# A running maximum for the widest tiles of a graph attention kernel, layer 1

## The chip, the cores and the metric

The kernel runs on one core of a Trainium2 chip. The time is device microseconds of one execution, smaller is better. The core has a matrix engine (PE, whose weight loads are shown apart as PEld), a vector engine (DVE), a scalar engine (ACT), a general engine (POOL), which in this kernel mostly issues gathers, and a queue engine (SP), all of which run their own instruction lists in order and wait for each other by semaphores. Sixteen DMA engines move data between the main memory and the on-chip memories (SBUF for data, PSUM for what the matrix engine sums).

## The reference

A graph has N = 10000 nodes and 170000 directed edges (80000 random ones in both directions, and a loop at each node). `x` has 768 numbers a node. Two graph attention layers follow each other, then a residual sum and a last layer norm. Layer 1 has 4 heads of 256 numbers, layer 2 one head of 768:

```
xl    = (x @ W).reshape(n, heads, out_ch)
e     = leaky_relu(alpha_src[src] + alpha_dst[dst], 0.2)
m     = segment_max(e, dst)
e     = exp(e - m[dst])
s     = segment_sum(e, dst)
alpha = e / (s[dst] + 1e-16)
out   = segment_sum(xl[src] * alpha[:, :, None], dst)      # then + bias
h     = relu(layer_norm(out)) + (x @ Wr1 + br1)            # layer 1
h     = layer_norm(out2) + (h1 @ Wr2 + br2)                # layer 2
x     = layernorm(x + h)
```

So every node takes a softmax over the edges that end in it, for each head, and a weighted sum of the source nodes' rows. Subtracting the maximum changes nothing but the range of the exponential; a softmax may therefore also be taken over groups of edges, if sums made with an older, smaller maximum are scaled by exp(old maximum − new maximum).

## The kernel before

A first stage (until about 900 us) computes `xl` and the two attention terms of every node, writes them as rows of 1033 floats into a table in main memory (`table1`: 1024 numbers, 4 + 4 attention terms, 1 rank), and sorts the nodes by their number of edges. Then layer 1 (about 900 to 3440 us) and layer 2 (to the end) work through 79 tiles of 128 nodes. A tile has a fixed number of slots, the most edges that a node of it may have: slot k of a tile is a gather of 128 table rows, one a partition, the k-th neighbour of each of the 128 nodes. The text calls such a gathered slot a **row** of the tile, and a tile's place in the order of work its **turn**. The slot counts, computed in `slot_counts`, rise from 8 in turn 0 to a peak in the middle and fall to 9 in turn 78. Turns 33 to 46 have 21, 22, 22, 23, 24, 26, 41, 27, 25, 24, 23, 22, 22 and 21 rows; no other turn has more than 21.

Rows live in a ring of `RING1 = 29` slots in SBUF, shared by consecutive turns (class `Ring`). `ring.fetch` issues the gather for ring position q on POOL as soon as position q − 29 has been used, in the order of work; line 424 is that gather.

A turn of at most 29 rows goes through the loop of `ordered_layer1` (lines 772 to 875):

- `weights_of(t)`: `logits` over all its rows (lines 477 to 489: sum of the attention terms, leaky ReLU, maximum over the rows, difference, `exp` on ACT, two small writes into `slots` and the ring), then `normalised` (doubled loop weight, sum, reciprocal, product; lines 496 to 502), then `summed`, in two halves: ACT scales a unit matrix by the weights (`diagonals`, line 727) and PE multiplies the first `on_pe(t)` rows (4 in the wide turns) with them into a PSUM tile `acc` (line 733).
- `weigh` adds the other rows to `acc` on DVE: one row in four as 4 instructions of 256 numbers, one a head, that multiply and add (line 519); of the other three ACT has scaled the row in the ring before (`multiply`, line 508), and DVE adds 1024 numbers in one instruction (line 515).
- The turn before is finished at the beginning of the loop: mean and deviation of its `acc` (`deviation`, lines 577 to 582), then `scaled` and the residual (lines 591, 593, 804), transposes, and products for layer 2.

The order in each engine's list is the order in which the code emits it. `weights_of(t + 1)` is a generator: its first piece, the logits, is emitted at row n − 3 of turn t (`LEAD` is 3), its second (normalisation and the first half of the sums) at row n − 2, the rest after the deviation at the beginning of turn t + 1. This needs all rows of turn t + 1 in the ring while 3 rows of turn t are still unused, hence the condition `SLOTS[t + 1] + LEAD <= ring.size`.

The one turn with 41 rows, turn 39, does not fit. It goes through `attend_parts`: 3 groups of 13, 14 and 14 rows with a running maximum; each group has its own logits, 4 rows on PE into a PSUM tile `sums`, the others into a tile `h` in SBUF, which is scaled by `fade = exp(top − new)` at each new group (line 543). Turn 39 isn't prepared during turn 38, nor turn 40 during turn 39.

Of the kernel before, what the change touches and what calls it, by code (L numbers as in the profile page):

```python
# [35 lines left out]
P = 128  # L36
# [14 lines left out]
ON_PE2 = 512  # L51
SHARE = 4
ON_PE1 = 4


def chunk_counts(n_edges):
# [23 lines left out]
def gnn_kernel(ctx, tc, x, x_cols, src, dst, src_col, dst_col, W1, a_src1, a_dst1, b1, g1, be1, Wr1, br1,  # L80
# [390 lines left out]
    def logits(small, ring, lo, hi, ad, heads, c, top=None):  # L471


        n = hi - lo
        e = small.tile([P, ring.size, heads], F32, name="e")[:, :n]
        for a, b, rows in ring.parts(lo, hi):
            nc.vector.tensor_tensor(e[:, a - lo:b - lo], rows[:, :, c + heads:c + 2 * heads],
                                    ad[:, None, :].to_broadcast([P, b - a, heads]), op=OP.add)
# [22 lines left out]
    def doubled(e, t):  # L501
        nc.vector.tensor_scalar(e[:, 0], e[:, 0], loops[:, TURNS[t]:TURNS[t] + 1], None, op0=OP.mult)

    def multiply(row, e, dh):

        for h in range(e.shape[1]):
            s = slice(h * dh, (h + 1) * dh)
            nc.scalar.activation(row[:, s], row[:, s], AF.Copy, scale=e[:, h:h + 1])  # L508

    def weigh(acc, row, e, dh, first=None, shared=False):  # L510


        if shared:
            c = e.shape[1] * dh
            nc.vector.tensor_add(acc[:, :c], acc[:, :c], row[:, :c])  # L515
            return
        for h in range(e.shape[1]):
            s = slice(h * dh, (h + 1) * dh)
            nc.vector.scalar_tensor_tensor(acc[:, s], row[:, s], e[:, h:h + 1],  # L519
                                           (acc if first is None else first)[:, s], op0=OP.mult, op1=OP.add)  # L520

    def attend_parts(small, ring, acc, h_, ad, heads, dh, t, summed, between):


        c = heads * dh
        groups = -(-SLOTS[t] * 2 // ring.size)
        cuts = [FIRST[t] + SLOTS[t] * g // groups for g in range(groups + 1)]
        top = total = sums = None
        nc.vector.memset(acc[:, :c], 0.0)
        for lo, hi in zip(cuts, cuts[1:]):  # L530
            e, new = logits(small, ring, lo, hi, ad, heads, c, top)
            if lo == FIRST[t]:
                doubled(e, t)
            part = small.tile([P, heads], F32, name="part")
            nc.vector.reduce_sum(part, e.rearrange("p k h -> p h k"), axis=AX.X)
            if top is not None:
                nc.vector.tensor_add(acc[:, :c], acc[:, :c], sums[:, :c])
                fade = small.tile([P, heads], F32, name="fade")
                nc.vector.tensor_sub(fade, top, new)
                nc.scalar.activation(fade, fade, AF.Exp)  # L540
                for h in range(heads):
                    s = slice(h * dh, (h + 1) * dh)
                    nc.vector.tensor_scalar(acc[:, s], acc[:, s], fade[:, h:h + 1], None, op0=OP.mult)
                nc.vector.tensor_mul(fade, total, fade)
                nc.vector.tensor_add(part, part, fade)
            top, total = new, part
            m = min(ON_PE1, hi - lo - 1)
            pe = lo if hi == cuts[-1] else hi - m
            steps = summed(pe, e[:, pe - lo:], m)
            sums = next(steps)  # L550
            if pe == lo:
                for _ in steps:
                    pass
            alone = [q for q in range(lo, hi) if not pe <= q < pe + m]
            for k, q in enumerate(alone):
                shared = k >= len(alone) // 3
                if shared:
                    multiply(ring.slot(q), e[:, q - lo], dh)
                if k == len(alone) // 3 + 1:
                    for _ in steps:  # L560
                        pass
                weigh(acc, ring.slot(q), e[:, q - lo], dh, shared=shared)
                ring.fetch(q + 1 + ring.size)
            ring.fetch(hi + ring.size)
            between.pop(0)()
        nc.vector.tensor_add(acc[:, :c], acc[:, :c], sums[:, :c])
        divided(small, h_, acc, total, None, heads, dh)

    def pieces(a, width):

# [112 lines left out]
    def ordered_layer1():  # L683
        nc.scalar.add_instruction(mybir.InstLoadActFuncSet(name=nc.get_next_instruction_name(), act_func_set_id=6, engine=nc.scalar.engine))
        with tc.tile_pool(name="b1", bufs=1) as pool, tc.tile_pool(name="small1", bufs=2) as small, \
# [32 lines left out]
            def on_pe(t):  # L718


                return min(max(SLOTS[t] // 2 - 5, 1), ON_PE1, SLOTS[t])

# [14 lines left out]

            def weights_of(t):

                n, m = SLOTS[t], on_pe(t)  # L740
                e, _ = logits(small, ring, FIRST[t], FIRST[t] + n, ring.slot(FIRST[t])[:, C1:C1 + H1], H1, C1)
                yield e
                normalised(small, e, H1, t)
                acc = ps_acc.tile([P, 2 * BANK], F32, name="acc")
                diagonals = pool.tile([P, ON_PE1 * H1, P], F32, name="diagonals")
                for lo, hi in ((0, min(m, 2)), (min(m, 2), m)):
                    summed(acc, diagonals, e, FIRST[t], lo, hi, m)
                    yield acc

            def shared(t, k):  # L750
                return (k - on_pe(t)) % SHARE > 0
# [20 lines left out]
            for t in range(NT + 1):  # L772
                live, events = t < NT, []
                n = SLOTS[t] if live else 0
                first = done = on_pe(t) if live else 0
                whole = live and n <= ring.size
                if whole and not ready:
                    ahead = weights_of(t)
                    ready += itertools.islice(ahead, 2)

                def multiplied(upto):
                    nonlocal done
                    while whole and done < min(upto, n):
                        if shared(t, done):
                            multiply(ring.slot(FIRST[t] + done), e[:, done], DH1)
                        done += 1

                if whole:
                    e, acc = ready
                if last:  # L790
                    r_before, means = last
                    stats = deviation(small, pieces(means[:, :C1], BANK))
                for _ in ahead:
                    pass
                if full is not None:
                    store(t - 2)
                moves = []
# [15 lines left out]
                    if live and t:  # L813
                        r = product(xT, wr1, C1, ps_r)

                if whole:
                    by_wr1()

                def to_layer2():
                    nonlocal full  # L820
# [20 lines left out]
                    while events and events[0][0] <= k:  # L841
                        events.pop(0)[1]()

                if live and not whole:
                    due(first + 1)
                    sums, acc = (ps_acc.tile([P, 2 * BANK], F32, name="acc") for _ in range(2))
                    ad = small.tile([P, H1], F32, name="ad")
                    nc.vector.tensor_copy(ad, ring.slot(FIRST[t])[:, C1:C1 + H1])

                    def some(q, e, m):  # L850
                        diagonals = pool.tile([P, ON_PE1 * H1, P], F32, name="diagonals")
                        for lo, hi in ((0, min(m, 2)), (min(m, 2), m)):
                            summed(sums, diagonals, e, q, lo, hi, m)
                            yield sums

                    h = pool.tile([P, C1], F32, name="h")
                    attend_parts(small, ring, h, acc, ad, H1, DH1, t, some,
                                 [by_wr1, lambda: due(n)] + [lambda: None] * n)
# [12 lines left out]
                due(DEGREES)  # L871
# [414 lines left out]
```

## Time and profile before

| | us |
|---|---|
| median of 3 runs | 5645.9 (5635.85 to 5646.04) |
| profiled execution | 5629.25, span 5627.4 |
| DVE busy in the span | 4288.7 (76%) |
| ACT / POOL / PE busy | 2810.9 / 3236.3 / 4889.5 |
| turns 33 to 45 (between the starts of their line 804) | 1879.92 to 2468.02, 588.1 |
| DVE busy in each 36 to 47 us turn there | 32 to 38 |
| turn 39 (41 rows) | 2128.45 to 2208.79, 80.34 |

Line 804 is emitted once a turn, so the time from one to the next is the length of a turn. A row of a timeline gives the start, the duration, the engine, the line, the operation, what it writes and reads, how often it follows itself, and in brackets how long the engine had been idle and what released it. Where equal instructions follow each other the duration is that of all of them.

### The profile page before, as it was taken

How to read it: one execution, taken by the hardware profiler on the slowest of the kernel's cores; microseconds unless marked ns; L12 is line 12 of the kernel's file. 1: busy time of each engine (PE TensorE's matmuls, PEld its weight loads, DVE VectorE, ACT ScalarE, POOL GpSimd, SP SyncE). 2: the span in 40 equal slices, each digit the busy share in tenths (PEclk: the TensorE clock that was granted, in tenths of full speed). 3: DMA queues.
4: the chain of work that ended last, by engine and by line, in shares of the span. 5: the costliest groups of instructions: out<-in, count | busy, mean ns of one | idle time of the engine just before them, and what ended most of it. 6: DMA issues, size and time to landing. Idle time of an engine off the chain costs nothing. (4 is left out here: it accounts for less than half of the span.)

```text
span 5627.4 us, 59568 instructions
## 1 busy us (share of the span) xinstructions
PE 4889.5 (87%) x15191; PEld 2895.8 (51%) x15191; DVE 4288.7 (76%) x7729; ACT 2810.9 (50%) x8184; POOL 3236.3 (58%) x3159
## 2 busy tenths in 40 slices
PE   8999996999999875789999999998887747788898
PEld 3444443555555543455555555565555534555565
DVE  5783344999998887888999995887676656767787
ACT  3443343777788776778877763332222222222232
POOL 2447364556666555566665543666565656666663
PEclk9999998999999987899999999998888878889999
DMA  4333626999999987899999986998888878888885
GB/s 155 122 99 87 92 89 243 327 338 350 361 363 364 347 318 263 317 346 357 366 356 354 337 292 246 330 337 313 294 301 286 282 242 291 307 300 305 304 328 201
DMA packets 474306, 1591.37 MB, mean 283 GB/s; under 512 B 118327, under 2 KB 122487, under 8 KB 473958
## 3 DMA queue, kind: packets, MB, share of 16 engines
q0 software_dynamic: 322384, 1286.62, 64.5%
q1 hardware_dynamic: 149520, 297.43, 15.7%
q10 hardware_dynamic: 2054, 3.42, 0.2%
q8 instruction: 128, 2.10, 0.1%
q14 instruction: 220, 1.80, 0.1%
HBM read 1431.80 MB, written 177.29 MB: 286 GB/s over the span
## 5 line engine op out<-in xcount | busy, mean ns | idle before, releaser
L424 POOL DMA_INDIRECT ring<-table,slots x2675 | 2655.8, 993 | 1791.0 <-issue 518.8
L519 DVE SCALAR_TENSOR_TENSOR acc<-ring,e,acc 128x512 f32<-128x512 f32 (+1 forms) x2530 | 1578.4, 624 | 148.0 <-PE acc L733 48.6
L508 ACT ACTIVATE ring<-ring,e 128x256 f32<-128x256 f32 x3284 | 1338.6, 508 | 1.4 <-issue 1.4
L515 DVE TENSOR_TENSOR acc<-acc,ring 128x1024 f32<-128x1024 f32 x801 | 985.6, 1230 | 71.4 <-DVE acc L519 1.4
L952 PE MATMUL big<-wr,w 128*128 128x512 f32 (+1 forms) x2464 | 878.9, 502 | 139.8 <-issue 137.9
L938 PE MATMUL big<-ring,diagonals 128*128 128x256 f32 x2754 | 742.1, 428 | 206.0 <-issue 159.2
L171 PE MATMUL big<-w,xT 128*128 128x512 f32 x1896 | 825.9, 597 | 27.0 <-DMA w<-in_W_dram 10.4
L171 PE MATMUL big<-wr,xT 128*128 128x512 f32 x1896 | 833.5, 596 | 0.2 <-issue 0.2
L826 PE MATMUL half<-w,hT 128*128 128x512 f32 (+1 forms) x2528 | 830.4, 486 | 0.0
L938 PEld LDWEIGHTS big<-ring,diagonals 128*128 128x128 f32 x2754 | 586.4, 216 | 364.9 <-issue 232.7
L952 PEld LDWEIGHTS big<-wr,w 128*128 128x128 f32 x2464 | 482.3, 197 | 499.9 <-issue 468.9
L937 ACT ACTIVATE diagonals<-ident,e 128x128 f32<-128x128 f32 x1377 | 424.3, 388 | 617.2 <-remote 227.0
L826 PEld LDWEIGHTS half<-w,hT 128*128 128x128 f32 x2528 | 477.8, 189 | 372.3 <-issue 333.2
L733 PE MATMUL acc<-ring,diagonals 128*128 128x256 f32 x1912 | 481.8, 410 | 209.4 <-ACT diagonals L727 203.8
L171 PEld LDWEIGHTS big<-w,xT 128*128 128x128 f32 x1896 | 362.0, 192 | 486.6 <-issue 466.3
L171 PEld LDWEIGHTS big<-wr,xT 128*128 128x128 f32 x1896 | 356.7, 192 | 420.6 <-issue 420.5
L733 PEld LDWEIGHTS acc<-ring,diagonals 128*128 128x128 f32 x1912 | 388.8, 206 | 295.4 <-ACT diagonals L727 225.0
L581 ACT ACTIVATE sd<-mv,eps 128x1 f32<-128x1 f32 x237 | 69.4, 293 | 709.9 <-DVE mv L579 398.4
L727 ACT ACTIVATE diagonals<-ident,e 128x128 f32<-128x128 f32 x956 | 293.0, 387 | 204.2 <-DVE e L499 171.9
L665 DVE TENSOR_TENSOR scr<-big,ad_b 128x1024 f32<-128x1024 f32 x79 | 96.7, 1224 | 379.9 <-ACT row L662 348.1
L670 POOL TENSOR_TENSOR row<-row,none 128x1024 f32<-128x1024 f32 x79 | 187.1, 2368 | 266.6 <-ACT row L662 264.6
L485 ACT ACTIVATE e<-e 128x68 f32<-128x68 f32 (+29 forms) x160 | 38.2, 239 | 567.0 <-DVE e L484 302.0
(173 smaller groups left out, 3635.0 us busy)
## 6 DMA issues: line engine op xcount, KB each, us to landing
ring<-table,slots POOLq DMA_INDIRECT x2675
table<-row SPq DMA_DIRECT2D x79, 516.0 KB
h_d<-hT SPq DMA_DIRECT2D x79, 512.0 KB
w<-h_d SPq DMA_DIRECT2D x77, 512.0 KB
table<-row SPq DMA_DIRECT2D x79, 385.0 KB
ring<-table SPq DMA_DIRECT2D x79, 385.0 KB
xT<-in_x_cols_dram SPq DMA_DIRECT2D x79, 384.0 KB
x_d<-xt SPq DMA_DIRECT2D x79, 384.0 KB
```

The costliest lines, as they stand in the source:

```text
L171: nc.tensor.matmul(p[:, c:e], aT[:, j, :], w[:, j, c:e], start=(j == 0), stop=(j == k - 1))
L424: nc.gpsimd.indirect_dma_start(out=to, out_offset=None, in_=table, in_offset=bass.IndirectOffsetOnAxis(ap=index, axis=0), **more)
L508: nc.scalar.activation(row[:, s], row[:, s], AF.Copy, scale=e[:, h:h + 1])
L515: nc.vector.tensor_add(acc[:, :c], acc[:, :c], row[:, :c])
L519: nc.vector.scalar_tensor_tensor(acc[:, s], row[:, s], e[:, h:h + 1], (acc if first is None else first)[:, s], op0=OP.mult, op1=OP.add)
L670: nc.gpsimd.tensor_add(row[:, :C1], row[:, :C1], b1_b)
L727: nc.scalar.activation(diagonals[:, k * H1 + i, :], ident, AF.Copy, scale=e[:, k, i:i + 1])
L733: nc.tensor.matmul(acc[:, c:d], diagonals[:, k * H1 + i, :], ring.slot(q + k)[:, c:d], start=(k == 0 and c % BANK == 0), stop=(k == m - 1 ...
L826: nc.tensor.matmul(q, hT[:, j, :], w2[:, j, c:c + q.shape[1]], start=(j == 0), stop=(j == K1 - 1))
L937: nc.scalar.activation(diagonals[:, k % G, :], ident, AF.Copy, scale=e[:, k, :])
L938: nc.tensor.matmul(to, diagonals[:, k % G, :], ring.slot(FIRST[t] + k)[:, ON_PE2:C2], start=False, stop=(k == n - 1), skip_group_check=True)
L952: nc.tensor.matmul(r[:, c:d], hT[:, j, :], wr2[:, j, c:d], start=False, stop=(j == K1 - 1 and d < C2), skip_group_check=True)
```

## The change

A threshold `PARTED = 22` is added. Tiles with 22 rows or more take their softmax in groups of rows: two groups, or three for the 41 rows. `cuts_of(t)` gives the borders: 11 for 22 and 23 rows, 13 for 24 to 27 rows, 13 and 27 for 41 rows (a border that would fall on a row not scaled by ACT moves on by one).

`weights_of` takes the logits of the first group only, and gives unnormalised weights; the sums of the four rows on PE go into `acc` with these. For each later group at row c it has two more pieces: the logits with the old maximum, and `fade`, emitted at row c − 8; then the running total, and for the last group the reciprocal, which is multiplied into the group's weights and into its `fade`, emitted at row c − 5. At row c `weigh` does acc = acc · fade + row, 4 instructions of 256 numbers, in place of one addition of 1024 numbers. All sums stay in the PSUM tile `acc`. `attend_parts` goes; turn 39 runs through the same loop as the others, and every turn is prepared during the one before it, whatever its size. Turns under 22 rows have one group and the instructions of before.

```diff
+PARTED = 22
@@ weigh
-    def weigh(acc, row, e, dh, first=None, shared=False):
+    def weigh(acc, row, e, dh, first=None, shared=False, fade=None):
+        if fade is not None:
+            for h in range(e.shape[1]):
+                s = slice(h * dh, (h + 1) * dh)
+                nc.vector.scalar_tensor_tensor(acc[:, s], acc[:, s], fade[:, h:h + 1], row[:, s],
+                                               op0=OP.mult, op1=OP.add)
+            return
@@ attend_parts is removed
-    def attend_parts(small, ring, acc, h_, ad, heads, dh, t, summed, between):
...
@@ weights_of
-                n, m = SLOTS[t], on_pe(t)
-                e, _ = logits(small, ring, FIRST[t], FIRST[t] + n, ring.slot(FIRST[t])[:, C1:C1 + H1], H1, C1)
-                yield e
-                normalised(small, e, H1, t)
+                n, m, at = SLOTS[t], on_pe(t), FIRST[t]
+                cuts = cuts_of(t)
+                ad = ring.slot(at)[:, C1:C1 + H1]
+                if len(cuts) > 2:
+                    own = ad
+                    ad = small.tile([P, H1], F32, name="ad")
+                    nc.vector.tensor_copy(ad, own)
+                e, top = logits(small, ring, at, at + cuts[1], ad, H1, C1)
+                yield {0: (e, None)}
+                if len(cuts) == 2:
+                    normalised(small, e, H1, t)
+                else:
+                    doubled(e, t)
+                    total = small.tile([P, H1], F32, name="total")
+                    nc.vector.reduce_sum(total, e.rearrange("p k h -> p h k"), axis=AX.X)
...
+                for lo, hi in zip(cuts[1:], cuts[2:]):
+                    e, new = logits(small, ring, at + lo, at + hi, ad, H1, C1, top)
+                    fade = small.tile([P, H1], F32, name="fade")
+                    nc.vector.tensor_sub(fade, top, new)
+                    nc.scalar.activation(fade, fade, AF.Exp)
+                    yield
+                    part = small.tile([P, H1], F32, name="part")
+                    nc.vector.reduce_sum(part, e.rearrange("p k h -> p h k"), axis=AX.X)
+                    nc.vector.tensor_mul(total, total, fade)
+                    nc.vector.tensor_add(total, total, part)
+                    top = new
+                    if hi == n:
+                        nc.vector.tensor_scalar(total, total, 1e-16, None, op0=OP.add)
+                        nc.vector.reciprocal(total, total)
+                        nc.vector.tensor_mul(fade, fade, total)
+                        nc.vector.tensor_mul(e, e, total[:, None, :].to_broadcast([P, hi - lo, H1]))
+                    yield lo, (e, fade)
+
+            def cuts_of(t):
+                n = SLOTS[t]
+                groups = 1 if n < PARTED else -(-2 * n // ring.size)
+                cuts = [n * g // groups for g in range(groups + 1)]
+                return [c + (0 < c < n and not shared(t, c)) for c in cuts]
@@ the loop over turns
-                for _ in ahead:
-                    pass
+                next(later, None)
...
-                if whole and t + 1 < NT and SLOTS[t + 1] + LEAD <= ring.size:
+                if live and t + 1 < NT:
                     ahead = weights_of(t + 1)
-                for k in range(n if whole else 0):
+                for k in range(n):
+                    if k + 2 * LEAD + 2 in cuts[1:-1]:
+                        next(later)
+                    if k + LEAD + 2 in cuts[1:-1]:
+                        lo, es_lo = next(later)
+                        es[lo] = es_lo
                     multiplied(k + 1 + LEAD)
                     if n - LEAD <= k < n - LEAD + 2:
                         ready += itertools.islice(ahead, 1)
                     if k >= first:
-                        weigh(acc, ring.slot(FIRST[t] + k), e[:, k], DH1, shared=shared(t, k))
+                        weights, fade = row_of(k)
+                        weigh(acc, ring.slot(FIRST[t] + k), weights, DH1, shared=shared(t, k), fade=fade)
```

More of the change, by code (lines that the diff above doesn't have):

```diff
@@ L520, in weigh @@
                                            (acc if first is None else first)[:, s], op0=OP.mult, op1=OP.add)
-    def attend_parts(small, ring, acc, h_, ad, heads, dh, t, summed, between):
[L525 to L552, printed above, removed]
-                    pass
[L554 to L567, printed above, removed]
     def pieces(a, width):
@@ L746, in weights_of @@
                 for lo, hi in ((0, min(m, 2)), (min(m, 2), m)):
-                    summed(acc, diagonals, e, FIRST[t], lo, hi, m)
+                    summed(acc, diagonals, e, at, lo, hi, m)
                     yield acc
+                for lo, hi in zip(cuts[1:], cuts[2:]):
[20 more added lines that the diff above has]
+                return [c + (0 < c < n and not shared(t, c)) for c in cuts]
             def shared(t, k):
@@ L775, in ordered_layer1, with row_of @@
                 first = done = on_pe(t) if live else 0
-                whole = live and n <= ring.size
-                if whole and not ready:
+                cuts = cuts_of(t) if live else []
+                if live and not ready:
                     ahead = weights_of(t)
                     ready += itertools.islice(ahead, 2)
+                def row_of(k):
+                    lo = max(c for c in es if c <= k)
+                    return es[lo][0][:, k - lo], es[lo][1] if k == lo else None
                 def multiplied(upto):
                     nonlocal done
-                    while whole and done < min(upto, n):
+                    while done < min(upto, n):
                         if shared(t, done):
-                            multiply(ring.slot(FIRST[t] + done), e[:, done], DH1)
+                            multiply(ring.slot(FIRST[t] + done), row_of(done)[0], DH1)
                         done += 1
-                if whole:
-                    e, acc = ready
+                later = iter(())
+                if live:
+                    es, acc = ready
+                    es, later = dict(es), ahead
                 if last:
@@ L792, in ordered_layer1 @@
                     stats = deviation(small, pieces(means[:, :C1], BANK))
-                for _ in ahead:
-                    pass
+                next(later, None)
                 if full is not None:
@@ L814, in by_wr1 @@
                         r = product(xT, wr1, C1, ps_r)
-                if whole:
-                    by_wr1()
+                by_wr1()
                 def to_layer2():
@@ L842, in due @@
                         events.pop(0)[1]()
[L844 to L858, printed above, removed]
                 ready = []
                 ahead = iter(())
-                if whole and t + 1 < NT and SLOTS[t + 1] + LEAD <= ring.size:
+                if live and t + 1 < NT:
                     ahead = weights_of(t + 1)
-                for k in range(n if whole else 0):
+                for k in range(n):
[4 more added lines that the diff above has]
+                        es[lo] = es_lo
                     multiplied(k + 1 + LEAD)
```

## The prediction

> **What bounds the kernel now.** The chain that ended last says nothing here: its pieces cover the last microsecond only. So I looked at the share of each engine, then at windows cut turn by turn, then at the waits of the turns that the change touches, then at the timeline of single turns. Windows first (columns: stretch, length, busy time and instruction count of PE, PEld, DVE, ACT, POOL, then the granted PE clock, the DMA share, GB/s):
>
> ```profile
> 1500.00:1600.00 100.00, 97.42 (x327) 57.96 (x327) 91.34 (x147) 80.54 (x218) 65.78 (x64) 1.00 0.99 365
> 1916.05:1955.65 39.60, 31.84 (x101) 19.58 (x100) 33.38 (x53) 28.87 (x79) 22.71 (x24) 0.87 0.91 334
> 2040.66:2087.15 46.49, 32.25 (x109) 20.15 (x108) 36.06 (x55) 32.06 (x87) 25.39 (x26) 0.85 0.82 300
> 2087.15:2128.45 41.30, 26.42 (x88) 15.05 (x86) 36.78 (x46) 30.01 (x77) 25.44 (x26) 0.84 0.99 367
> 2128.45:2208.79 80.34, 50.00 (x169) 34.54 (x170) 61.02 (x132) 53.09 (x152) 49.29 (x42) 0.78 0.59 206
> ```
>
> In narrow turns (first line) DVE, PE and DMA are nearly full together. In the wide turns (turns 34, 37, 38, 39) nothing is: DVE and DMA wait for each other. The waits of turns 33 to 45 (columns: who waits for whom, total us, times, longest):
>
> ```profile
> POOL ring L424 <- DVE e L502: 54.8, 11, 7.3
> DVE e L477 <- DMA ring<-table,slots: 37.9, 12, 5.3
> DVE acc L519 <- PE acc L733: 20.6, 12, 4.9
> ```
>
> The second line is the stall in question; 1.8 us more is put down to "issue", so 39.7. Turn 37 shows the mechanism, DVE above and POOL below:
>
> ```profile
> 2068.68 2.06 DVE L519 SCALAR_TENSOR_TENSOR acc<-ring,e,acc 128x256 f32<-128x256 f32 x4
> 2070.66 0.16 DVE L477 TENSOR_TENSOR e<-ring 128x8 f32<-128x8 f32 x1
> 2076.17 0.26 DVE L477 TENSOR_TENSOR e<-ring 128x96 f32<-128x96 f32 x1 [5.35 <-DMA ring<-table,slots]
> 2077.86 1.21 DVE L515 TENSOR_TENSOR acc<-acc,ring 128x1024 f32<-128x1024 f32 x1
> ...
> 2071.02 0.99 POOL L424 DMA_INDIRECT ring<-table,slots  x1 [1.11 <-DVE e L477]
> 2079.33 0.99 POOL L424 DMA_INDIRECT ring<-table,slots  x1 [7.33 <-DVE e L502]
> ```
>
> The logits of turn 38 need all its 26 rows; the last goes into the slot that DVE gave free at 2070.7, its gather starts at 2071.02, and DVE stands until 2076.17. Meanwhile no slot comes free, so POOL and then the DMA engines stand too. Outside turns 33 to 45 this wait is nearly absent (2.4 us from 1100 to 1879, none from 2504 to 3400). DVE's own chain is then what sets a turn, and I sum on that chain.
>
> **What goes.** (a) In the new order the logits of turn t+1 at row n−3 need only its first 11 or 13 rows, released some 14 rows (21 us) earlier. The 39.7 us go, except in turn 45, whose successor has 21 rows and is still taken whole: of its 2.72 I keep 1.5. −38.2.
>
> Is the wait only moved to the second group's logits? They need row n−1. Its slot comes free several rows before the end of turn t−1; then follow the first logits of turn t, statistics and scaling (4.43, line 577 to 804), line 804 (1.22), and for a border at 13 also the PE wait and row 4. At 1.53 a row (6.11 for four) this is 16.8 to 18.8 us in nine turns, 14 to 16 in turns 38 to 40, and 10.7 for the third group of turn 39. The trace shows from gather start to the waiting logits 5.2 us above, 7.9 in turn 34 (1936.18 to 1944.07) and 9.9 in turn 45 (2446.67 to 2456.57, DMA share 0.95). So it has landed; only the third group of turn 39 is near.
>
> (b) The 20.6 us for PE stand between line 804 and the first weighted row. With a border at 11 (turns 34, 35, 36, 43, 44, 45) the second logits are emitted at row 3, before the first weighted row, and fill this gap: the smaller of 1.70 (their price below) and the gap (1.10, 1.78, 1.78, 2.40, 2.14, 0.72), together −8.6. (c) Turn 40 has 4.90 there because its sums started late; prepared ahead it should have the mean of the others, 1.4: −3.5.
>
> Sum of what goes: 50.3.
>
> **What is added.** Turn 39 of before already shows a later group's small instructions on DVE:
>
> ```profile
> 2149.71 0.21 DVE L477 TENSOR_TENSOR e<-ring,ad 128x56 f32<-128x56 f32 x1
> 2151.22 0.25 DVE L535 TENSOR_REDUCE part<-e 128x4 f32<-128x56 f32 x1
> 2152.52 0.15 DVE L539 TENSOR_TENSOR fade<-new 128x4 f32<-128x4 f32 x1
> 2154.31 0.16 DVE L544 TENSOR_TENSOR fade<-part,fade 128x4 f32<-128x4 f32 x1
> 2154.50 0.16 DVE L545 TENSOR_TENSOR part<-part,fade 128x4 f32<-128x4 f32 x1
> ```
>
> Logits 1.51 (2149.71 to 2151.22) and the difference for `fade` 0.19 (together the 1.70), the partial sum 0.17, two operations on the total 0.28: 2.15. The last group adds four small instructions, 0.82 by the pitch of lines 497 to 499 (0.20). The row at the border costs 4 instructions (2.17 from start to start) and not one (1.31): 0.86. A second group is 3.83. The first group costs 1.74 (2132.87 to 2134.61) and 0.20 for the copy of `ad`; the whole-tile logits and normalisation that it replaces took 2.85. Net 1.94 + 3.83 − 2.85 = 2.92 a turn; eleven turns with two groups: +32.1.
>
> Turn 39 alone: before, its own DVE work lies between 2129.59 and 2194.04, 64.4 us, with a clearing of `h`, scalings by line 543, additions of `sums` and some 7 us of waits for ACT in it. After: 1.94, a middle group 3.01, a last 3.83, 37 rows in 57.2 (27 at 1.31, 10 at 2.17) and the PE gap of 1.4: 67.4. +3.0.
>
> ACT gets 13 `exp` of e and 13 of `fade`, at 0.25 and 0.20; it is busy 32 of 46 us in turn 37 and its list reaches them after DVE has the logits, so 0. If that cover were gone, the idle 0.27 seen before line 543 would be paid at each. PE does the same products, fewer for turn 39. POOL and SP issue the same DMAs: the gathers and the writes to `table2`, `h1_d` and `x_d` are only passed by small DVE work, and POOL waits for rows as before. DMA needs share times length, 503 us in turns 33 to 45 of 573 left: 0.88, under the 0.98 that narrow turns reach.
>
> **Sum.** 50.3 gone, 35.1 added, net −15.2 on the profiled execution's 5629.25: 5614.05. That execution lies under all three timed runs; scaled to their median of 5645.9, 5630.7.
>
> **A rule that speaks against it.** The row: an operation of 128x4 takes 0.16 and a DVE instruction of 256 numbers 0.49, against 1.23 for 1024. The Trainium skill, "VectorE: DVE Perf Modes", section "The TRN2 errata — SBUF-src ops pay a fixed extra latency per instruction", says that every instruction pays a fixed latency and advises tiles of 512 elements or more; halving tiles of 88 elements does the reverse. Its formula of (N+151)/0.96 ns would make the four instructions at a border 1.70, 0.47 less than the row, and the sum 6 us better. I take the row.
>
> **Rivals and bounds.**
> 1. Slower: the stall moves with the logits. If each of the 13 later groups waits 3.2 us (37.9 / 12, today's mean), 41.6 comes back: +26.4, 5672 on the median's scale. Break-even is 1.2 us a group, slower by 0.2% from 2.0. For it: the DMA share is 0.91 before and the turns get shorter, so gathers may queue longer. Against: it needs landings beyond 15 us, and the longest seen is 9.9.
> 2. Nothing measurable: a later group costs 3.8 net where I have 2.92 (0.05 for each of six more semaphore waits, two bubbles of 0.27 for `exp`), +11, gain 4: 5642. For it: line 543 did wait for ACT. Against: in the new order three rows lie between.
> 3. More: all 2.72 of turn 45 goes (1.2), PE gaps of the turns with a border at 13 shrink as the PE clock (0.78 to 0.88 there, 1.00 in narrow turns) recovers (5), a group costs 2.5 (5): gain 27, 5619.
> 4. DMA takes over as the bound: it would have to top out at 0.88; turn 38 shows 0.99. I count it with rival 1.
>
> **How the numbers follow.** A difference of 0.2% (11.3 us) is about what a measurement of this kernel can tell from none. Chances: gain between 11 and 20 us 0.45, over 20 (rival 3) 0.15, between 0 and 11 (rival 2) 0.22, a loss under 11 0.03, a larger loss (rivals 1 and 4) 0.15. Faster 0.60, same 0.25, slower 0.15. The likeliest case alone spans 5619 to 5642. The range goes a little past rival 3, to 5614, for the spread of 10 us in the timed runs, and up to 5656, break-even plus 10, half of rival 1.
>
> **What would show it.** Right: no DMA wait at line 477 in turns 33 to 44; logits of the later group between line 804 and the first line 519 in turns 34 to 36 and 43 to 45; turns 34 and 35 at 39 us, 37 at 43, 38 at 47 (longer than before), 39 at 73, 40 at 48; POOL's wait for line 502 gone; POOL's gathers in turn 39 back at 0.99. Wrong: a DMA wait at the second line 477 of a turn, ACT waits before the border row, or wide turns that stay at their lengths with DVE busier.

## The result

The changed kernel took a median of 5607.26 us (5602.11 to 5621.37), the kernel before 5641.66 us beside it; the ratio is 0.9949, 95% interval 0.9932 to 0.9965. Two more comparisons on other chips gave 0.9969 (0.9956 to 0.9982) and 0.9960 (0.9947 to 0.9973). On 5641.66 us these are 29, 17 and 23 us. (The ratio on record is not that of the two medians, which are 34.4 us apart.) The change is faster, as forecast, and by more than the 15.2 us forecast: 5607.26 lies below the range of 5614 to 5656.

The two profiled spans differ by 27.1 us (5627.4 and 5600.3). Turns 33 to 45 take 561.9 us in place of 588.1, so 26.2 of it is there. The rest is code that did not change: the first stage, the other turns of layer 1 and layer 2 differ by −2.8, −4.6 and +6.4 us. That is within its scatter: in the traces of all the runs below that leave this code alone, the other turns of layer 1 take 1879 to 1886 us and layer 2 takes 2193 to 2222.

Windows of the changed kernel, cut at the starts of line 804, which has the same number in it (columns as before: stretch, length, busy time and count of PE, PEld, DVE, ACT, POOL, granted PE clock, DMA share, GB/s); these are turns 34, 37, 38 and 39:

```profile
1908.02:1946.24 38.22, 31.62 (x104) 19.36 (x103) 35.20 (x66) 28.95 (x81) 22.85 (x23) 0.91 0.97 348
2024.60:2067.27 42.67, 31.17 (x100) 19.06 (x99) 38.00 (x71) 32.24 (x89) 24.70 (x26) 0.84 0.93 327
2067.27:2113.84 46.57, 32.81 (x109) 20.28 (x108) 41.18 (x77) 33.87 (x93) 27.55 (x28) 0.85 0.93 325
2113.84:2184.73 70.89, 31.66 (x104) 19.50 (x103) 64.76 (x117) 51.76 (x139) 42.27 (x43) 0.71 0.71 234
```

DVE is busy longer in each of them (turn 37: 38.00 in place of 36.06), and the turns are shorter, except turn 38, which now also prepares turn 39. The DMA share rose from 0.91 to 0.97 in turn 34 and from 0.82 to 0.93 in turn 37.

The gain is not spread evenly. Of the 26.2 us, turn 33 has 2.1, turns 34 to 37 have 11.9, and turns 38 to 40 have 9.9 together. Turns 41 to 45, where the tiles become narrower again, have only 2.3. (Against the second profile of the kernel before, these three groups have 9.3, 10.1 and 1.1.) In turns 41 to 45 the removed waits (15.9 us) are hardly longer than the added work (13.6).

The waits of the same turns (who waits for whom, total, times, longest; line 526 is the old 519, 478 the old 477, 503 the old 502, 693 the old 733, 425 the old 424):

```profile
POOL ring L425 <- DVE e L503: 23.5, 13, 2.5
...
DVE acc L526 <- PE acc L693: 6.4, 7, 1.8
...
DVE e L478 <- DMA ring<-table,slots: 0.2, 1, 0.2
```

DVE's DMA waits went from 37.9 to 0.2, its waits for PE from 20.6 to 6.4, POOL's for line 502 from 54.8 to 23.5. The end of turn 37, where before DVE stood 5.35 us:

```profile
2054.89 2.06 DVE L526 SCALAR_TENSOR_TENSOR acc<-ring,e,acc 128x256 f32<-128x256 f32 x4
2056.86 0.16 DVE L706 COPY ad<-ring 128x4 f32<-128x4 f32 x1
2057.06 0.17 DVE L478 TENSOR_TENSOR e<-ring,ad 128x8 f32<-128x8 f32 x1
2057.43 0.20 DVE L478 TENSOR_TENSOR e<-ring,ad 128x44 f32<-128x44 f32 x1 [0.20 <-DMA ring<-table,slots]
...
2058.79 1.21 DVE L522 TENSOR_TENSOR acc<-acc,ring 128x1024 f32<-128x1024 f32 x1
```

The logits of turn 38 now take the first 13 rows only (8 + 44 columns, four for each row), and DVE waits 0.20 us for them. What this costs is seen in turn 35 (22 rows, border at 11):

```profile
1946.24 1.22 DVE L804 SCALAR_TENSOR_TENSOR h<-h,big 128x1024 f32<-128x1024 f32 x1
1947.38 0.27 DVE L478 TENSOR_TENSOR e<-ring,ad 128x8 f32<-128x8 f32 x2
...
1948.97 0.11 DVE L723 TENSOR_TENSOR fade<-new 128x4 f32<-128x4 f32 x1
1949.00 2.06 DVE L526 SCALAR_TENSOR_TENSOR acc<-ring,e,acc 128x256 f32<-128x256 f32 x4
1951.16 1.23 DVE L522 TENSOR_TENSOR acc<-acc,ring 128x1024 f32<-128x1024 f32 x1
1952.30 0.22 DVE L727 TENSOR_REDUCE part<-e 128x4 f32<-128x44 f32 x1
...
1953.39 0.20 DVE L735 TENSOR_TENSOR e<-e,total 128x44 f32<-128x44 f32 x1
1953.50 2.56 DVE L522 TENSOR_TENSOR acc<-acc,ring 128x1024 f32<-128x1024 f32 x2
...
1960.95 2.29 DVE L517 SCALAR_TENSOR_TENSOR acc<-acc,fade,ring 128x256 f32<-128x256 f32 x4
```

The second group's logits stand directly behind line 804, and no wait is left. In turn 35 of before DVE waited 1.78 us for PE at this place:

```profile
1955.65 1.22 DVE L804 SCALAR_TENSOR_TENSOR h<-h,big 128x1024 f32<-128x1024 f32 x1
1958.65 2.06 DVE L519 SCALAR_TENSOR_TENSOR acc<-ring,e,acc 128x256 f32<-128x256 f32 x4 [1.78 <-PE acc L733]
```

Seven small operations follow behind row 5 (1952.30 to 1953.50), and the row at the border takes 2.29 in place of 1.23.

For every run below, the length of turns 33 to 45 is split in DVE's waits (the sum of the idle times in the brackets of its timeline) and the rest, called **occupied**. This is the measure that a few us can be read from; whole executions of one kernel on one chip scatter by up to 33 us, and the kernel before has medians of 5607.57 to 5641.66 us in the comparisons on different chips, so the ratios are only taken within a chip.

| kernel | turns 33 to 45 | waits of DVE | occupied | ratio to before, interval |
|---|---|---|---|---|
| before | 588.1 | 70.9 | 517.2 | |
| before_again | 586.2 | 69.0 | 517.1 | 0.9999 (0.9988 to 1.0010) |
| changed | 561.9 | 7.6 | 554.4 | 0.9949 (0.9932 to 0.9965) |
| again | 562.3 | 8.0 | 554.3 | 0.9969 (0.9956 to 0.9982) |
| again_b | 563.5 | 9.1 | 554.4 | 0.9960 (0.9947 to 0.9973) |
| read_last | 584.1 | 28.7 | 555.5 | 0.9994 (0.9984 to 1.0005) |
| only_two | 579.1 | 49.6 | 529.5 | 0.9987 (0.9975 to 0.9999) |
| late | 569.9 | 16.1 | 553.8 | 0.9972 (0.9961 to 0.9983) |
| no_ahead | 570.6 | 15.5 | 555.1 | 0.9975 (0.9964 to 0.9986) |
| twice | 580.0 | 9.5 | 570.5 | 0.9987 (0.9976 to 0.9999) |
| parted20 | 567.8 | 10.9 | 556.9 | 1.0006 (0.9995 to 1.0016) |
| early | 557.3 | 2.3 | 555.0 | 0.9959 (0.9944 to 0.9974) |
| early_b | 557.5 | 2.3 | 555.1 | 0.9957 (0.9944 to 0.9970) |
| split | 562.4 | 11.6 | 550.8 | 0.9958 (0.9941 to 0.9975) |
| early_split | 554.8 | 3.3 | 551.5 | 0.9949 (0.9932 to 0.9965) |

So the change takes 63.3 us of waits away and adds 37.2 us of work, and the occupied time repeats within 0.15 us between the profiles of one kernel.

### The profile page after: what moved, and what is told of

Read it like the earlier page. It is cut to its first block, busy times and chain, and to the rows that moved or that the text cites. A ratio compares the mean times of both kernels' runs of the same rounds, so it can differ in the third digit from the quotient of the medians.

```text
span 5600.3 us, 59697 instructions
## 1 busy us (share of the span) xinstructions
PE 4875.2 (87%) x15124; PEld 2874.6 (51%) x15127; DVE 4318.0 (77%) x7908; ACT 2813.4 (50%) x8202; POOL 3229.9 (58%) x3159
## 5 line engine op out<-in xcount | busy, mean ns | idle before, releaser
L526 DVE SCALAR_TENSOR_TENSOR acc<-ring,e,acc 128x256 f32<-128x256 f32 (+1 forms) x2570 | 1597.9, 622 | 130.5 <-PE acc L693 29.5
L522 DVE TENSOR_TENSOR acc<-acc,ring 128x1024 f32<-128x1024 f32 x815 | 1002.7, 1230 | 69.0 <-issue 0.9
L942 PE MATMUL big<-wr,w 128*128 128x512 f32 (+1 forms) x2464 | 901.3, 509 | 166.6 <-issue 164.7
L928 PE MATMUL big<-ring,diagonals 128*128 128x256 f32 x2754 | 728.7, 423 | 181.1 <-issue 150.7
L693 PE MATMUL acc<-ring,diagonals 128*128 128x256 f32 x1848 | 460.6, 406 | 217.7 <-ACT diagonals L687 212.6
L693 PEld LDWEIGHTS acc<-ring,diagonals 128*128 128x128 f32 x1848 | 370.1, 203 | 300.8 <-ACT diagonals L687 235.8
L486 ACT ACTIVATE e<-e 128x52 f32<-128x52 f32 (+27 forms) x171 | 40.4, 236 | 562.1 <-DVE e L485 229.1
```

Source lines behind the costliest of these rows:

```text
L693: nc.tensor.matmul(acc[:, c:d], diagonals[:, k * H1 + i, :], ring.slot(q + k)[:, c:d], start=(k == 0 and c % BANK == 0), stop=(k == m - 1 ...
L928: nc.tensor.matmul(to, diagonals[:, k % G, :], ring.slot(FIRST[t] + k)[:, ON_PE2:C2], start=False, stop=(k == n - 1), skip_group_check=True)
L942: nc.tensor.matmul(r[:, c:d], hT[:, j, :], wr2[:, j, c:d], start=False, stop=(j == K1 - 1 and d < C2), skip_group_check=True)
```

## The experiments

**Is it the execution or the kernel?** The changed kernel twice more, and the kernel before once more, unedited.

> The changed kernel once more, beside the others of this set. Ratio to before 0.9949 as measured (5600.3 us profiled); turns 33 to 45 together 562 us against 588 before, each within 0.5 us of the first profile. If the gain were an accident of one placement or one execution, the turns would differ by more.

> The changed kernel a third time, beside the next three. Turns 33 to 45 at 562 +- 1; ratio to before between the two measured, 0.9949 and 0.9969.

> The kernel before, profiled a second time, to see what of the difference between the two traces is only the difference between two executions. Expected: turns 33 to 45 within 3 us of the 588.1 of the first trace, DVE's waits there within 3 us of 70.9; layer 2, whose code does not change, differing by up to 12 us between executions, as it does between the four traces of the changed kernels. If turns 33 to 45 came out near 575, the 26 us between the traces would be chance, and the 15.2 predicted would be right.

The turns repeat: 561.9, 562.3 and 563.5 against 588.1 and 586.2. Chance is out. The last of the three is half a us above its forecast; 1.2 us of its difference to the first are in turn 33, which is not parted and waits 0.21, 0.90 and 1.38 us for PE in the three profiles. The ratios of whole executions scatter more (0.9949, 0.9969, 0.9960). The second span of before is 5635.7 in place of 5627.4 with a layer 1 of the same length (2471.4 and 2471.6): the difference is in layer 2, 2218.1 and 2208.7.

**Is it the wait for the last rows?** One copy of four numbers from the last row, ahead of the first group's logits:

```diff
                     nc.vector.tensor_copy(ad, own)
+                    if n + LEAD <= ring.size:
+                        seen = small.tile([P, H1], F32, name="seen")
+                        nc.vector.tensor_copy(seen, ring.slot(at + n - 1)[:, C1:C1 + H1])
```

> The changed kernel, but the first logits of a tile with 22 to 26 rows are preceded by a copy of 4 numbers from the tile's last row, so DVE waits for the landing of that row as before; nothing else differs. Theory (the gain is DVE no longer waiting for the last rows of the next tile): the waits of the ten turns 33 to 37 and 40 to 44 come back, 29.7 us in the trace of before, and ten copies of 0.2 us: +32 us against the changed kernel, the whole gain and a little more; about 5632 us profiled, ratio to before 1.000 to 1.002. Rival (the gain is the new path of the 41-row tile and the filled gap after line 804): +2 us, ratio 0.995. Rival (slots free earlier, the waits come back smaller because DMA no longer falls behind): between, +10 to +20.

The end of its turn 37, and the waits of its turns 33 to 45:

```profile
2069.14 0.16 DVE L706 COPY ad<-ring 128x4 f32<-128x4 f32 x1
2073.82 0.17 DVE L709 COPY seen<-ring 128x4 f32<-128x4 f32 x1 [4.52 <-DMA ring<-table,slots]
2073.90 0.17 DVE L478 TENSOR_TENSOR e<-ring,ad 128x8 f32<-128x8 f32 x1
```

```profile
DVE seen L709 <- DMA ring<-table,slots: 17.6, 7, 4.5
DVE acc L526 <- PE acc L693: 8.8, 9, 2.3
```

A copy of 0.17 us brings the wait back, 4.52 us in turn 37, and makes the turns 21.8 us longer than in again, beside it. The ratio goes from 0.9969 to 0.9994: most of the gain is gone. For the tiles of 22 to 26 rows the mechanism is shown. The size was not the +32 that I expected: 17.6 us came back where the trace of before had 29.7 in these ten turns. That is nearer to the third reading, waits that come back smaller, and a little above its +10 to +20. In turns 42 to 44 almost nothing came back. DVE's occupied time in them is 2.2 to 3.0 us longer than before, which gives the last row more time to land; whether this is the reason or the DMA engines fall behind less, no run separates.

**Is it the 41-row tile alone?**

```diff
-PARTED = 22
+PARTED = 27
```

> Threshold 27: only the tiles of 27 and 41 rows go in groups. Theory: turns 33 to 37 and 41 to 45 return to their lengths of before (together 16 us longer), turn 40 waits again for all rows of turn 41 (+4 to +5); turns 38 and 39 keep 46.6 and 70.9. Together +20 us against the changed kernel, ratio to before 0.998 to 0.999. Rival (the 41-row tile's path is the gain): within 5 us of the changed kernel, 0.995.

Waits of its turns 33 to 45:

```profile
DVE e L478 <- DMA ring<-table,slots: 27.1, 10, 5.2
DVE acc L526 <- PE acc L693: 17.1, 13, 2.3
```

579.1 us, 16.8 more than again; the turns 33 to 37 are back at their lengths of before within 0.8 us each, turn 39 stays at 71.7. The new path of the 27 and 41-row tiles is worth 7 to 9 us (579.1 against 586.2 and 588.1), the parting of the 22 to 26-row tiles the rest. The expected +20 was 3 too many: turn 38 (26 rows) is not parted at this threshold either and takes 43.2, not the 46.6 that I expected it to keep. And of the 16.8 us nothing to speak of lies in turns 41 to 45: they take 204.5 us here and 204.1 in again. The parting of 22 to 26 rows gains where the tiles become wider, not where they become narrower.

**Does the second group's work fill the wait for PE?** The logits of a later group two rows later, behind the first weighted row, the rest one row later:

```diff
-                    if k + 2 * LEAD + 2 in cuts[1:-1]:
+                    if k + 2 * LEAD in cuts[1:-1]:
                         next(later)
-                    if k + LEAD + 2 in cuts[1:-1]:
+                    if k + LEAD + 1 in cuts[1:-1]:
```

> The logits of a later group are emitted 6 rows before the border instead of 8, the rest 4 rows before it instead of 5; in the turns with a border at 11 they then stand behind the first weighted row. Theory (they fill DVE's wait for PE there): a DVE wait for PE of 1 to 2.4 us comes back in turns 34, 35, 36, 43, 44 and 45, +5 to +9 us, ratio 0.996 to 0.9965; no change in the turns with a border at 13. Rival (the wait for PE went for another reason, the PE clock or an earlier start of the sums): the waits stay away, +0 to +2 us.

Waits of DVE in its turns 33 to 45:

```profile
DVE acc L526 <- PE acc L693: 14.5, 13, 2.1
```

The wait is back in all six turns with a border at 11, 0.56 to 1.30 us each (less than the 1 to 2.4 expected), 5.6 together; the thirteen turns are 7.6 us longer than in again, of which 1.7 are in turns 37 and 38. Whole executions (0.9972 and 0.9969) don't show so little.

**And where it is not yet filled?** The second group's logits at row 3 in every parted turn:

```diff
-                    if k + 2 * LEAD + 2 in cuts[1:-1]:
+                    if len(cuts) > 2 and k == first - 1 or k + 2 * LEAD + 2 in cuts[2:-1]:
```

> The second group's logits are always emitted at row 3, before the first weighted row, also in the turns with a border at 13 (37 to 42); the third group of turn 39 as before. Theory (they cost nothing while DVE waits for PE): the waits of 0.6 to 1.7 us in turns 37 to 42, 5.9 us together, go: turns 33 to 45 at 556 to 557; a ratio 0.1% better, too little for the timing. Rival (the last row hasn't landed so early): a DMA wait appears at the second group's logits in turns 38 to 40, and the sum stays at 562 or grows by up to 5.

> The version with the second group's logits at row 3 in all parted turns, a second time, beside the changed kernel on one chip. Turns 33 to 45 at 557 (5 less than the changed kernel), ratio 0.001 better than the changed kernel's; the intervals will overlap.

DVE's waits in the turns of early:

```profile
DVE acc L526 <- PE acc L693: 1.2, 3, 0.8
DVE h L804 <- PE acc L693: 0.5, 1, 0.5
...
DVE e L478 <- DMA ring<-table,slots: 0.2, 1, 0.2
```

557.3 and 557.5 us, 4 to 6 less, and no new DMA wait though the last rows are asked for two rows earlier. This beats the changed kernel in the turns; the ratios (0.9957 beside 0.9960 on one chip) cannot tell.

**What is the preparation of turns 39 and 40 worth?** The old condition back:

```diff
-                if live and t + 1 < NT:
+                if live and t + 1 < NT and SLOTS[t + 1] + LEAD <= ring.size:
```

> Turns 39 and 40 are not prepared during the turn before (the old condition on the ring's size is back), all else as in the changed kernel. Theory: the sums of the first rows start late, DVE waits about 4.9 us for PE at the start of turns 39 and 40 in place of 0.6: +8 to +9 us, 570 to 571 together. Rival (the whole 15.2 us that turns 39 and 40 became shorter come from the preparation): +15. Rival (the preparation is worth nothing, the PSUM sums and the missing waits for ACT did it): under +2.

DVE's waits for PE at the start of turns 39 and 40:

```profile
2125.57 2.06 DVE L526 SCALAR_TENSOR_TENSOR acc<-ring,e,acc 128x256 f32<-128x256 f32 x4 [3.75 <-PE acc L693]
...
2200.35 2.07 DVE L526 SCALAR_TENSOR_TENSOR acc<-ring,e,acc 128x256 f32<-128x256 f32 x4 [4.05 <-PE acc L693]
```

The changed kernel has 0.57 and 0.64 there. Turns 33 to 45 are 8.6 us longer than in the first trace. This is the theory's number, but only 7.0 of it are in turns 39 and 40; the rest is in turns 37 and 38, where DVE waits 1.4 us longer for PE than in the first trace.

**Does DVE's own chain set the turns?** Six more small operations for each later group:

```diff
+                    for _ in range(2):
+                        spare = small.tile([P, H1], F32, name="spare")
+                        nc.vector.reduce_sum(spare, e.rearrange("p k h -> p h k"), axis=AX.X)
+                        nc.vector.tensor_mul(spare, spare, fade)
+                        nc.vector.tensor_add(spare, spare, fade)
                     yield lo, (e, fade)
```

> Each later group gets six more small DVE operations in a chain (twice a reduction over its weights, a product and a sum, into a tile that nobody reads), about 1.2 us by the durations 0.23, 0.15, 0.16 and the pitch of 0.2. Theory (DVE's own chain sets the wide turns): 13 groups, +14 to +16 us in turns 33 to 45, 576 to 578 together. Rival (slack somewhere takes it up, DMA or PE being the bound after the change): under +8. If small operations between dependent additions are partly free: about +12.

Occupied +16.1 us, turns +18.0 against the first trace, the timed ratio 0.9987. For 13 groups the 16.1 are 1.24 us each, as priced; the turns are 2 us above the forecast, because DVE's waits grew by 1.9 as well. No slack takes the work up: after the change DVE's own chain sets these turns, with the few waits for PE that are left.

**Does parting pay where there is no wait?**

```diff
-PARTED = 22
+PARTED = 20
```

> Threshold 20: ten more turns in two groups (29 to 33 and 46 to 50, 20 or 21 rows), in which DVE waits little for DMA. Theory (a group costs DVE 2.45 us; it pays only by the waits it removes): +24.5, less the 7.7 us of PE waits and the 3.2 us of DMA waits that these turns have in the changed kernel: +13 to +14 us in turns 28 to 51, ratio 0.998 to 0.9995. Rival (DMA is the bound of these turns, share 0.98, and DVE has room): +0 to +4. Rival (shorter waits let DMA run ahead for all turns): a gain.

Turns 28 to 33 and 46 to 51 take 431.9 us, 24.8 more than the 407.1 in again_b: all of the gain is lost (1.0006). I expected +13 to 14. Waits of DVE from 1650 to 2630 us (turns 26 to 50):

```profile
DVE acc L526 <- PE acc L693: 11.6, 10, 2.2
DVE part L727 <- ACT e L486: 6.6, 10, 1.0
DVE e L478 <- DMA ring<-table,slots: 0.9, 4, 0.2
```

With a border at 10 the partial sum (line 727) follows one weighted row after the logits, and DVE now waits for ACT's exponential, 6.6 us in the ten turns. DVE's waits in the twelve turns stay at 12.1 (13.6 before the edit) and its occupied time rises by 26.3. The price per group holds (2.6 us here); the waits that should have paid for it were replaced by another.

**Why is a group cheaper than I priced it?** The same small operations in two places, the reciprocal and the products one row after the partial sum:

```diff
                     top = new
+                    yield
                     if hi == n:
...
                     if k + LEAD + 2 in cuts[1:-1]:
+                        next(later)
+                    if k + LEAD + 1 in cuts[1:-1]:
                         lo, es_lo = next(later)
```

> The small operations of a later group after its logits are emitted in two places, the partial sum and the total at the row 5 before the border, the reciprocal and the two products one row later; same instructions. My price of a group was 0.47 us a turn too high (2.92 against 2.45 measured). Theory (an addition into acc waits for the one before, start to start 1.31, but an operation that doesn't use acc starts 1.14 after it, so each place where small operations come between rows gains 0.17 to 0.2): one more place in 12 of the 13 groups, -2 us in turns 33 to 45, 560 together. Rival (the price was wrong for another reason): no change, or +1 for the second interruption.

Turn 35 of split, to be read against turn 35 above:

```profile
1958.59 1.23 DVE L522 TENSOR_TENSOR acc<-acc,ring 128x1024 f32<-128x1024 f32 x1
1959.73 0.22 DVE L727 TENSOR_REDUCE part<-e 128x4 f32<-128x44 f32 x1
...
1960.06 0.23 DVE L729 TENSOR_TENSOR total<-total,part 128x4 f32<-128x4 f32 x1
1960.21 1.22 DVE L522 TENSOR_TENSOR acc<-acc,ring 128x1024 f32<-128x1024 f32 x1
1961.35 0.15 DVE L733 TENSOR_SCALAR total<-total 128x4 f32<-128x4 f32 x1
...
1961.83 0.20 DVE L736 TENSOR_TENSOR e<-e,total 128x44 f32<-128x44 f32 x1
1961.94 1.23 DVE L522 TENSOR_TENSOR acc<-acc,ring 128x1024 f32<-128x1024 f32 x1
1963.20 2.06 DVE L526 SCALAR_TENSOR_TENSOR acc<-ring,e,acc 128x256 f32<-128x256 f32 x4
```

Three additions and seven small operations take 4.61 us from the first to line 526 (1958.59 to 1963.20), against 4.94 in the changed kernel (1951.16 to 1956.10). An addition is followed after 1.14 by an operation that does not use `acc`, but after 1.34 by the next addition (two in a row take 2.57, one 1.23; the 1.31 above is the mean of a block of three, whose last is followed after 1.26 by the multiply-and-add of the next row). So 0.20 of the 0.33 are in the additions; the rest is in the small operations, 1.07 us in two places and 1.20 in one. In all, occupied time falls by 3.6 us, 0.30 for each of the 12 groups. The turns themselves gained only 1.1 against again_b where I expected 2, since DVE's waits grew by 2.6, 1.9 of it for PE. Whether the gain is real or only moved was tried with the waits filled:

> Both edits together: the second group's logits at row 3, and the later small operations in two places. In the run with the second edit alone DVE's occupied time in turns 33 to 45 fell by 3.6 us, but its waits for PE grew by 2.5, so the turns gained 1.1. Theory (more interruptions shorten DVE's own chain by 0.3 us each, and the waits for PE only hid it): with the waits filled the 3.6 show whole, 557.4 - 3.6 = 553 to 555. Rival (the interruptions only move time from rows to waits): 556 to 558.

554.8 us, inside the theory's 553 to 555 and 2.5 less than early; two thirds of the 3.6 arrive. Turn 33, whose code is the same in both, is 0.9 longer by a wait for PE; turns 34 to 45 are 3.5 shorter. In these turns it is the best version found. In whole executions it takes 5573.72 us beside 5607.57 for the kernel before on its chip, a ratio of 0.9949, which cannot be told from the changed kernel's three.

## Why the prediction was right or wrong

- **The bound and the mechanism** were right: 0.2 us of DMA waits is left at the first logits, none moved to the later groups (rival 1 is out; even the third group of turn 39 did not wait). read_last shows for the tiles of 22 to 26 rows that the wait for the last row is what was removed, and twice that DVE's chain sets the turns. One reading of the windows was wrong: in turn 38 of before, which prepared no other turn and had no DMA wait, the DMA share is 0.99, so not all of the four wide turns had room everywhere.
- **The forecast lengths** of 39, 43, 47, 73 and 48 us for turns 34, 37, 38, 39 and 40 came out as 38.2, 42.7, 46.6, 70.9 and 47.0: all a little high. The working implied 12.5 us of waits left (1.5 for DMA, 9.9 for PE, 1.1 of others) and 43.3 us more work; measured were 7.6 and 37.2. The 11 us between 15.2 and 26.2 are 6.1 of work that I priced too high and 4.9 of waits that I kept.
- **The step that failed most** is "Net 1.94 + 3.83 − 2.85 = 2.92 a turn". Over the nine turns that have a second group of their own and prepare one for the next (34 to 37, 40 to 44), occupied time rose by 2.23 to 2.71, mean 2.45; eleven of them make 5.2 of the 6.1 us. In turn 35 the terms came out so: the second group's logits 1.54 for 1.70, its later operations 1.00 for 1.27, the border row 1.06 for 0.86, the first group 1.81 for 1.94 (1.42 from 1974.03 and 0.39 from 1976.57), and what they replace 2.93 for 2.85; that is 2.48, and DVE's occupied time in this turn rose by 2.47. I priced every small operation by its pitch and each row by its full time, and left out that an interruption shortens the operation before it. A parted turn has two more interruptions than a whole one; in turn 35 they shorten row 5 from 1.34 to 1.14 and line 804 from 1.22 to 1.14, 0.28 together, and split shows the same 0.20 when one more is added.
- **The waits left.** (b) filled the gap and was 1.3 too small: all 9.9 us went in the six turns, where I had 8.6, and late brings 5.6 back. (c) was 0.8 too small, 0.64 us are left in turn 40 and not 1.4. Of the 9.9 us that I left for PE, 6.4 are there: less in turns 37 (0.93 for 2.36), 39, 40, 43 and 44, a little more in 38 and 41. Why the PE wait of a turn with a border at 13 differs is not settled; in turn 38 it is 1.76, 1.68 and 1.81 in the three profiles, 2.13 in late. The 1.5 us kept for turn 45 did not come: DVE's own work in this turn is 3.6 us longer, which may let the 21 rows land; in only_two, where turn 45 has the work of before, 1.05 of the wait is there.
- **POOL.** Its wait for line 502 was to go; nearly half is left, 13 waits of at most 2.5 us. They cost DVE nothing, as its waits show. Its gathers in turn 39 are back at 0.99 us (median; 1.02 before), as said.
- **The rule on small operations** was rightly not used for the price. The formula of the Trainium skill ("VectorE: DVE Perf Modes", section "The TRN2 errata — SBUF-src ops pay a fixed extra latency per instruction") is given there for an fp32 addition of two tensors, and fits those here (1.22 us by it for 1024 numbers, 1.23 measured). For the four multiply-and-adds at the border it would give an estimate of 1.70 us. They took 2.28 to 2.29, more than the 2.06 of the other rows' four. That more and smaller operations cost time agrees with parted20, which loses; in turns 33 to 40 the removed waits outweigh it.
- **Rivals 2 to 4.** Rival 2 is out: ACT made no bubble with borders at 11 and 13 (it did with 10), and its 0.05 us for a semaphore wait is shown by no run. Rival 3 has the size that came, 27: its 2.5 us a group and the whole wait of turn 45 were right (the sum kept 1.5 of it, so this term is 1.5 and not 1.2). Its third term came in part by luck: 3.5 us of PE waits went beyond the sum, but not by the PE clock, which in turns 34 to 45 stood at 0.82 to 0.91 before and after, and in turn 39 went from 0.78 to 0.71. Rival 4 is out: the DMA share rose to 0.97.
- **The size and the range.** 15.2 us are a ratio of 0.9973, inside the second interval, at the edge of the third and outside the first; the turns' 26.2 lie inside the first and the third. The median of 5607.26 lies 23.4 us under the 5630.7 forecast: 11.0 are the error of the sum, 4.2 are the kernel before, whose median is 5641.66 and not 5645.9 in this comparison, and the other 8.2 are outside these turns, which I put down to the scatter of whole executions. With the 26.2 us of the turns alone it would have been 5619.7, so that it fell below 5614 is in part chance. The range was too narrow below all the same. It took the price's lower end only into rival 3, and gave the scatter of whole executions 5 us, where comparisons of the same two kernels differ by 12 us.

## What to carry to other kernels

Where a batch of small work needs a whole tile of gathered rows while the ring still holds the last tile, splitting it so that it only needs the early rows removes the wait; it pays where the removed wait is longer than the second batch costs, 2.5 us here. That was so while the tiles became wider (9.3 to 11.9 us gained in turns 34 to 37); it was about even while they became narrower (turns 41 to 45), and a loss at 20 and 21 rows. One threshold on the number of rows does not say this; the waits of each turn do. Put the second batch where the engine waits for another one anyway. Price small operations between dependent additions as a group and from a place where they already stand so, not one by one.

## What was not expected of the hardware

- On DVE, an addition of 1024 numbers into the same PSUM tile starts 1.34 us after the one before it, an independent small operation after 1.14. The later group's small operations are 0.30 us cheaper in two places than in one (split).
- The multiply-and-add with `acc` as the scaled operand takes 2.28 us for four instructions of 256 numbers (line 517), with the row as the scaled operand 2.06 (line 526).
- A wait that was removed and then brought back is smaller than it was (17.6 of 29.7 us). The added work on the waiting engine gives the DMA engines more time; that this is the reason is likely but not shown.
